# First layer of experts 1 to 6 by fifteen block products for eighteen, with the weight loads of experts 1 to 3 behind the first gathered rows

## The chip, the cores and the metric

The kernel runs on one core of a Trainium2 chip. A core has five engines with an instruction queue each: TensorE (PE, with its weight loads shown apart as PEld), VectorE (DVE), ScalarE (ACT), GpSimd (POOL) and SyncE (SP). Each takes its instructions in order; they wait for each other through semaphores. Matmuls and transposes go to PSUM, eight banks of 128 x 512 floats; everything else on the core lies in SBUF. The metric is the device time of one execution in microseconds (us), as the median of several runs.

## The reference

`x` is 1250 tokens of 768 floats. A graph part (two attention layers over 41,250 edges) and a linear-attention part (`mix`) are added to it; then comes a mixture of eight experts, with the best two of a gate for each token:

```python
x = x + gnn(xn, edges) + mix(xn)          # xn: layer norm of x
t = layernorm(x)
gate = t @ Wg + bg
scores, idx = top_k(gate, 2)
h = gelu(einsum('td,edh->eth', t, W1) + b1)      # W1: 8 x 768 x 384
y = einsum('eth,ehd->etd', h, W2) + b2           # W2: 8 x 384 x 768
comb = sum(one_hot(idx, 8) * scores)
out = x + einsum('te,etd->td', comb, y)
```

All of it is in 32-bit floats. The kernel computes an expert for the tokens that chose it, not for all.

## The kernel before, in words

The parts run one after another: edges and features, six attention heads, keys and values of `mix`, and then a stage over five pairs of token tiles (from about 580 to 865 us) that ends the tokens: queries, output projections, the sum, layer norm and the gate. That stage writes each finished tile twice: to `out`, and, normalised and with its gates, to a buffer in device memory, `xl_d` (L937 and L951). At its end the numbers of the tokens of each expert are known, as columns of `idx` of 128 tokens each (L1049).

The expert stage follows. Each expert gets three columns, 384 tokens, from the code; columns beyond these are handled at the end (`other`). For expert e:

- `gather` (L1060) fetches the rows of three columns from `xl_d` with an indirect DMA on the GpSimd queue each (`xg`, three buffers), turns them with 18 PE transposes into six banks `px`, and copies these to `xsT` on VectorE (L1075). It also copies the gates of the tokens.
- `inner` (L1081) is the first layer: for each of three blocks f of 128 hidden features, six matmuls of 384 columns (weights block stationary, tokens moving) into a bank `ph`, and a gelu with bias on ScalarE to `hT` (L1092). That is 18 matmuls. A 32-bit matmul [...]shows as two records in the profile. Expert 0 is done for its first column alone and then for the other two.
- `give` (L1095), once for each column j, is the second layer: ScalarE multiplies the bias row with the gates (`gb`, two buffers), PE does two halves of three matmuls into two banks `py`, VectorE makes `ys = py * gate + gb` (L1108, two buffers), and an indirect DMA on the GpSimd queue adds the rows to `out` (L1110). Each of these scatter-adds waits for the one before it to land, since they write the same tensor.

In the loop (L1160) the order of the code is: `inner` of e, `gather` of e + 1, three `give` of e, then the loads for later. `spare` holds the second bias rows of two experts; the row of e + 2 is loaded when the last `gb` of e is done (L1175). The weights lie in a ring of four buffers `w` (`expert`, L745, two loads of 1152 KB on the SP queue: first layer L748, second layer L750), shared with the weight matrices of the stage before. Expert 0 takes the first buffer that comes free there; experts 1 to 3 take the others in L1050 and L1051, as the last products of that stage are done with them. The weights of e + 4 are loaded when the second layer of e has been computed (L1177).

PSUM is split into pools: two banks for `px`, two for `ph`, four for `py`.

The order in the queues is not quite that of the code. The framework that builds the program has a scheduler, which moves an instruction ahead of others on its engine where it reckons that the engine would wait otherwise; the matmuls of `py` between the transposes `px` are its work, for instance.

`xnT` (128 x 7500 floats) and `kept` (128 x 7920) hold features and weights of the earlier stages. The expert stage of the kernel before doesn't use them.

Of the kernel before, what the change touches and what calls it, by code (L numbers as in the profile page):

```python
# [27 lines left out]
F32 = mybir.dt.float32  # L28
# [12 lines left out]
KC = D // 128  # L41
# [19 lines left out]
def row_bcast(ap, parts):  # L61

    n = 1
    for s in ap.shape:
        n *= s
    return bass.AP(tensor=ap.tensor, offset=ap.offset, ap=[[0, parts], [1, n]])


@with_exitstack
def gps_block(ctx: ExitStack, tc: tile.TileContext, x, src, dst, norm_g, norm_b, W1, a_src1, a_dst1,  # L70
# [671 lines left out]

    fp = ctx.enter_context(tc.tile_pool(name="fp", bufs=1, side="right"))

    def expert(w1, w2, b2, b):  # L745

        t = wt.tile([128, KC, D], F32, name="w", bufs=4).rearrange("p c f -> p (c f)")
        nc.sync.dma_start(t[:, :KC * FF].rearrange("p (c f) -> p c f", c=KC),  # L748
                          w1.rearrange("(c p) f -> p c f", p=128))
# [18 lines left out]
    with ExitStack() as rs:  # L768
# [290 lines left out]

    def gather(rows, e):  # L1060

        got = []
        for r in rows:
            xg = sp.tile([128, D + NE], F32, name="xg", bufs=3)
            nc.gpsimd.indirect_dma_start(xg, None, xl_d, bass.IndirectOffsetOnAxis(r, 0))
            got.append(xg)
        xT = sp.tile([128, KC, FIX * 128], F32, name="xsT")
        gates = sp.tile([128, FIX], F32, name="gates")
        for j, xg in enumerate(got):
            for a in range(2):  # L1070
                px = x_p.tile([128, 512], F32, name="px")
                for c in range(3):
                    o = (3 * a + c) * 128
                    nc.tensor.transpose(px[:, c * 128:(c + 1) * 128], xg[:, o:o + 128], ident)  # L1074
                nc.vector.tensor_copy(xT[:, 3 * a:3 * a + 3, j * 128:(j + 1) * 128],  # L1075
                                      px[:, :384].rearrange("p (b n) -> p b n", b=3))
            at = slice(D + e, D + e + 1) if isinstance(e, int) else bass.ds(e + D, 1)
            nc.vector.tensor_copy(gates[:, j:j + 1], xg[:, at])
        return xT, gates

    def inner(w, xT, bias, a=0, b=FIX, hT=None):  # L1081

        if hT is None:
            hT = sp.tile([128, FC, FIX * 128], F32, name="hT")
        n = slice(a * 128, b * 128)
        for f in range(FC):
            ph = h_p.tile([128, 512], F32, name="ph")
            for c in range(KC):
                o = c * FF + f * 128
                nc.tensor.matmul(ph[:, n], w[0][:, o:o + 128], xT[:, c, n], start=c == 0,  # L1090
                                 stop=c == KC - 1)
            nc.scalar.activation(hT[:, f, n], ph[:, n], AF.Gelu, bias=bias[:, f])  # L1092
        return hT

    def give(w, hT, j, rows, gates):  # L1095
# [4 lines left out]
        ys = sp.tile([128, D], F32, name="ys")  # L1100
        for k in range(2):
            half = slice(k * 384, (k + 1) * 384)
            py = y_p.tile([128, 512], F32, name="py")
            for f in range(FC):
                o = KC * FF + f * D + k * 384
                nc.tensor.matmul(py[:, :384], hT[:, f, j * 128:(j + 1) * 128], w[:, o:o + 384],  # L1106
# [44 lines left out]
    for vals, add, row in ((place, float(NV), v_row), (which, 0.0, e_row)):  # L1151
        pick = fp.tile([128, NE], F32, name="pick", bufs=2)
        nc.vector.tensor_mul(pick, vals, mine)
        one = fp.tile([128, 1], F32, name="one", bufs=2)
        nc.vector.tensor_reduce(one, pick, AX.X, ALU.add)
        pr = h_p.tile([128, 512], F32, name="ph")
        nc.tensor.transpose(pr[:1, :128], one, ident)
        nc.vector.tensor_scalar(row, pr[:1, :128], add, None, op0=ALU.add)

    for e in range(NE - 1):  # L1160
        xT, gates = ahead
        bias = fb1T[:, :, e:e + 1]
        if e:
            hT = inner(ring[e], xT, bias)
        else:
            hT = inner(ring[e], xT, bias, 0, 1)
            inner(ring[e], xT, bias, 1, FIX, hT)
        ahead = gather(fixed(e + 1), e + 1)
        if e == NE - 2:
            ee, more_rows, more_bias, more_w = first  # L1170
            more_xT, more_gates = gather([more_rows], ee)
        for j, rows in enumerate(fixed(e)):
            give(ring[e], hT, j, rows, gates[:, j:j + 1])
        if e + 2 < NE:
            nc.sync.dma_start(spare[e % 2], row_bcast(fb2[e + 2], 128))  # L1175
        if e + 4 < NE:
# [53 lines left out]
```

## Time and profile before

| | |
|---|---|
| Median of 3 runs | 1097.52 us (1096.05 to 1099.54) |
| The profiled execution's own time | 1097.82 us |
| Its span, first to last instruction | 1096.1 us |
| PE busy, share of the span | 1031.0 us, 94% |
| VectorE busy | 705.8 us, 64% |
| ScalarE busy | 359.9 us, 33% |
| GpSimd busy | 78.8 us, 7% |
| DMA, over the span | 79.51 MB, 73 GB/s |

In the expert stage alone, from 901.00 to 926.50 us (one expert): PE 25.50 us of 25.50, VectorE 6.91, ScalarE 4.55, GpSimd 7.67, DMA 202 GB/s.

Names of tiles in the profile are those of the code, without buffer numbers. `L1090` is line 1090 of the kernel before. A group line has the count, the busy time with the mean of one in ns, and the idle time of the engine just before these instructions with what ended it. `SPq` is the queue of DMA issues of SyncE. The granted clock of PE is given as a share of full speed. The chain of work that ended last is followed backwards from the last instruction, at each step to what released it.

### The profile page before, as it was taken

How to read it: one execution, taken by the hardware profiler on the slowest of the kernel's cores; microseconds unless marked ns; L12 is line 12 of the kernel's file. 1: busy time of each engine (PE TensorE's matmuls, PEld its weight loads, DVE VectorE, ACT ScalarE, POOL GpSimd, SP SyncE). 2: the span in 40 equal slices, each digit the busy share in tenths (PEclk: the TensorE clock that was granted, in tenths of full speed). 3: DMA queues.
4: the chain of work that ended last, by engine and by line, in shares of the span. 5: the costliest groups of instructions: out<-in, count | busy, mean ns of one | idle time of the engine just before them, and what ended most of it. 6: DMA issues, size and time to landing. Idle time of an engine off the chain costs nothing.

```text
span 1096.1 us, 12392 instructions
## 1 busy us (share of the span) xinstructions
PE 1031.0 (94%) x4630; PEld 701.6 (64%) x4630; DVE 705.8 (64%) x1460; ACT 359.9 (33%) x548; POOL 78.8 (7%) x106
## 2 busy tenths in 40 slices
PE   6999999999999999988999999999999499999996
PEld 5876666587878879544555555656665376666674
DVE  7866684697897957769687958686855522222321
ACT  4612226372728373283833121112110111111121
POOL 2000000000000000000001000000000122223321
PEclk9999999999999999999999999999999699999998
DMA  5060000000000002000035002021144847777534
GB/s 161 29 211 19 29 15 1 1 1 1 1 1 1 1 1 87 1 0 1 15 142 153 1 15 71 20 65 43 58 153 132 274 116 221 213 213 203 116 58 59
DMA packets 35412, 79.51 MB, mean 73 GB/s; under 512 B 7078, under 2 KB 15416, under 8 KB 35348
## 3 DMA queue, kind: packets, MB, share of 16 engines
q1 hardware_dynamic: 29588, 58.90, 16.8%
q0 software_dynamic: 5760, 19.78, 8.5%
q8 instruction: 37, 0.61, 0.2%
q14 instruction: 27, 0.22, 0.1%
HBM read 60.33 MB, written 18.34 MB: 72 GB/s over the span
## 4 chain that ended last, share of the span: by engine, by line
PE 73%; DVE 20%; DMA 2%; ACT 1%; issue 1%; POOL 0%; DVEq 0%; POOLq 0%; ACTq 0%
PE s L863 19%; PE mm L648 9%; PE ph L1090 9%; PE py L1106 8%; PE mm L477 8%; DVE scr L569 6%; DVE w L589 5%; DVE w L590 5%; PE ag L602 3%; PE mm L924 2%; PE ag L624 2%; PE ec L398 2%; PE mm L452 2%; PE px L1074 2%; PE rb L558 1%; PE mm L662 1%
## 5 line engine op out<-in xcount | busy, mean ns | idle before, releaser
L602 PE MATMUL ag<-kept,w 125*125 125x198 f32 x800 | 137.5, 333 | 5.1 <-DVE w L590 4.8
L602 PEld LDWEIGHTS ag<-kept,w 125*125 125x125 f32 x800 | 133.5, 188 | 9.0 <-DVE w L590 9.0
L1106 PE MATMUL py<-w,hT 128*128 128x384 f32 x300 | 100.9, 486 | 0.0
L1090 PE MATMUL ph<-xsT,w 128*128 128x384 f32 (+2 forms) x432 | 99.9, 390 | 0.0
L589 DVE TENSOR_TENSOR w<-v,w 125x1250 f32<-125x1250 f32 x60 | 86.3, 1453 | 6.0 <-ACT w L587 5.4
L648 PE MATMUL mm<-Wv_sb,xnT 128*125 128x384 f32 x240 | 85.6, 489 | 4.8 <-DVE kvacc L668 4.8
L1090 PEld LDWEIGHTS ph<-xsT,w 128*128 128x128 f32 x432 | 68.9, 191 | 30.3
L569 DVE CUSTOM_DVE_ANT_0 scr<-ss_row,mask 125x1250 bf16<-125x1250 f32 x60 | 87.2, 1453 | 1.6 <-ACT ss_row L560 1.2
L477 PE MATMUL mm<-Wg,xnT 128*125 128x400 f32 x240 | 87.7, 505 | 0.2 <-ACT xnT L367 0.2
L590 DVE SCALAR_TENSOR_TENSOR w<-w,AT 125x1250 f32<-125x1250 f32 x60 | 86.4, 1454 | 0.4
L588 ACT ACTIVATE v<-dn_row,sl 125x1250 f32<-125x1250 f32 x60 | 79.3, 1333 | 17.4 <-DVE w L589 16.9
L648 PE MATMUL mm<-Wk_sb,xnT 128*125 128x384 f32 x240 | 85.0, 487 | 0.0
L1108 DVE SCALAR_TENSOR_TENSOR ys<-py,gates,gb 128x384 f32<-128x384 f32 x50 | 30.3, 616 | 79.3 <-PE py L1106 54.7
L1106 PEld LDWEIGHTS py<-w,hT 128*128 128x128 f32 x300 | 55.1, 190 | 33.1
L1075 DVE COPY xsT<-px 128x384 f32<-128x384 f32 x50 | 25.8, 552 | 73.3 <-PE px L1074 73.3
L648 PEld LDWEIGHTS mm<-Wv_sb,xnT 128*125 128x125 f32 x240 | 42.5, 187 | 31.4 <-DVE kvacc L668 6.9
L477 PEld LDWEIGHTS mm<-Wg,xnT 128*125 128x125 f32 x240 | 42.5, 188 | 26.5 <-ACT xnT L367 0.9
L1099 ACT ACTIVATE gb<-spare,gates 128x768 f32<-128x768 f32 x24 | 22.4, 935 | 112.4 <-DVE ys L1108 94.8
L587 ACT ACTIVATE w<-up_row,s 125x1250 f32<-125x1250 f32 x40 | 53.2, 1331 | 17.7 <-PE ag L602 17.6
L648 PEld LDWEIGHTS mm<-Wk_sb,xnT 128*125 128x125 f32 x240 | 42.0, 187 | 22.7 <-issue 1.8
L863 PE MATMUL s<-w,xnT 128*125 128x384 f32 x150 | 55.4, 489 | 0.0
L863 PE MATMUL s<-w 128*125 128x384 f32 x150 | 53.9, 491 | 0.0
(328 smaller groups left out, 1515.1 us busy)
## 6 DMA issues: line engine op xcount, KB each, us to landing
w<-in_L_ffn_W_dram SPq DMA_DIRECT2D x18, 1152.0 KB
xt<-in_x_dram SPq DMA_DIRECT2D x20, 336.0 KB
out_dram<-xt SPq DMA_DIRECT2D x10, 336.0 KB
xl_d<-xl SPq DMA_DIRECT2D x10, 336.0 KB
spare<-in_L_ffn_b_dram SPq DMA_DIRECT2D x8, 384.0 KB
W_sb<-in_L_gnn_W_dram SPq DMA_DIRECT2D x1, 2304.0 KB
Wk_sb<-in_L_mix_Wk_dram SPq DMA_DIRECT2D x1, 2304.0 KB
Wv_sb<-in_L_mix_Wv_dram SPq DMA_DIRECT2D x1, 2304.0 KB
```

Source lines behind the costliest of these rows:

```text
L477: nc.tensor.matmul(ps[:PT, :2 * (CG + 2)], xnT[:, c, t * PT:(t + 1) * PT], Wg1[:, c, 2 * k:2 * k + 2].rearrange("p h c -> p (h c)"), start ...
L569: nc.vector.tensor_tensor_reduce(scr, ss_row, mask[:, t], 1.0, 0.0, ALU.mult, ALU.max, top[:, t:t + 1])
L587: nc.scalar.activation(w, up_row, AF.Exp, bias=ss[:, st:st + 1])
L588: nc.scalar.activation(v, dn_row, AF.Exp, bias=sl[:, st:st + 1])
L589: nc.vector.tensor_tensor(w, v, w, op=ALU.max)
L590: nc.vector.scalar_tensor_tensor(w, w, 2.0, AT[:, st, :N], op0=ALU.min, op1=ALU.mult)
L602: nc.tensor.matmul(ag[:, t // 2, o:o + CG], w[:, t * PT:(t + 1) * PT], gw[:, st, hd], start=st == 0 and t % 2 == 0, stop=st == NT - 1, ski ...
L648: nc.tensor.matmul(ps[:PT, :384], xnT[:, c, t * PT:(t + 1) * PT], w[:, c, half], start=c == 0, stop=c == KC - 1)
L863: nc.tensor.matmul(ps, left[:, c], right[:, c], start=start and c == 0, stop=c == n - 1, skip_group_check=True)
L1090: nc.tensor.matmul(ph[:, n], w[0][:, o:o + 128], xT[:, c, n], start=c == 0, stop=c == KC - 1)
L1106: nc.tensor.matmul(py[:, :384], hT[:, f, j * 128:(j + 1) * 128], w[:, o:o + 384], start=f == 0, stop=f == FC - 1)
L1108: nc.vector.scalar_tensor_tensor(ys[:, half], py[:, :384], gates, gb[:, half], op0=ALU.mult, op1=ALU.add)
```

## The change

Split the first layer of an expert into blocks: W1, transposed, is 3 x 2 blocks (three blocks of 128 hidden features, two halves of 384 input features), and the gathered tokens are 2 x 3 (two halves of input features, three columns of 128 tokens). The plain product of these takes 18 products of blocks, each of them three matmuls. The change does it with fifteen: eleven sums and differences of the weight blocks (`WAYS[0]`) and eleven of the token blocks (`WAYS[1]`) are made first, each 128 x 384 floats; each product multiplies one block or sum of weights by one of tokens; and the nine blocks of the result are sums of products (`PRODUCTS`).

- `weight_sums` and `token_sums` make the sums on VectorE. They lie in 33 slots of `xnT` and `kept`: two sets of eleven for weights, one for tokens.
- `inner15` does the products, three matmuls of 128 columns each (L1124 of the kernel after). Five of the fifteen are added onto a bank that already holds another product. A product's first use in a block of `hT` is a copy on ScalarE (`=`, or `=-` with the sign turned), each further one an addition or subtraction on VectorE from the bank. When all is done, three gelus run over `hT` in place. It is called for experts 1 to 6; experts 0 and 7, and the columns at the end, keep `inner`.
- The `xsT` copies of experts 1 to 7 go from VectorE to ScalarE.
- The three PSUM pools of the stage become one, `e_p`, of eight banks in turn.
- The loads of experts 1 to 3 are issued behind the gather of expert 0: VectorE first copies a gathered gate into two elements of the buffer, so that the load of that buffer waits for the copy.

In the code, the sums for the weights of e + 1 stand between the products of e, those of expert 1 between the `give` of expert 0, and the token sums of e + 1 ahead of the `give` of e. In the program as built, the scheduler has moved the weight sums of one expert up: those of experts 1 and 2 both stand in expert 0's part, those of e + 2 between the products of e for e = 1 to 4, and none between those of 5 and 6.

```diff
+WAYS = ((("12", 5, 1, 6), ("13", 3, 1, 4), ("9", 1, -1, "13"), ("14", 3, -1, 1), ("15", 2, -1, "12"),
+         ("7", 1, 1, "15"), ("3", 2, -1, 6), ("8", 4, 1, 5), ("-2", 2, 1, "9"), ("1", 5, -1, 3),
+         ("5", 6, -1, 4)),
+        (("4", 5, -1, 2), ("2", 4, 1, 6), ("9", "2", -1, 3), ("14", 1, -1, "9"), ("7", 1, 1, 2),
+         ("11", 6, -1, 3), ("15", "7", -1, 5), ("3", "15", -1, 4), ("8", 3, -1, 5), ("1", 3, -1, 2),
+         ("5", 6, -1, 5)))
+PRODUCTS = (
+    ("6", None, 1, 1, (1, "="), (2, "=-")),
+    ("10", None, 2, 4, (1, "+"), (3, "=-"), (7, "=")),
+    ("12", None, "12", 5, (8, "="), (9, "=")),
+    ("4", None, 5, "4", (8, "-"), (5, "=-")),
+    ("9", None, "9", "9", (4, "=-"), (3, "-")),
+    ("14", "6", "14", "14", (4, "+")),
+    ("13", None, "13", 3, (3, "+"), (6, "=")),
+    ("7", "12", "7", "7", (2, "+")),
+    ("11", None, 4, "11", (4, "-"), (6, "+"), (9, "+")),
+    ("3", "4", "3", "3", (7, "+")),
+    ("8", None, "8", "8", (5, "-")),
+    ("2", None, "-2", "2", (3, "+")),
+    ("15", None, "15", "15", (2, "-"), (7, "-")),
+    ("1", "13", "1", "1", (5, "+")),
+    ("5", "8", "5", "5", (9, "+")))
...
-    def expert(w1, w2, b2, b):
+    def expert(w1, w2, b2, b, behind=None):
         t = wt.tile([128, KC, D], F32, name="w", bufs=4).rearrange("p c f -> p (c f)")
+        if behind is not None:
+            nc.vector.tensor_copy(t.rearrange("p (a f) -> p a f", a=2)[:1, :, 0],
+                                  behind.to_broadcast([1, 2]))
...
-        for e in range(1, 4):
-            ring.append(expert(fW1[e], fW2[e], fb2[e] if e < 2 else None, spare[e % 2]))
...
-    x_p = ctx.enter_context(tc.tile_pool(name="x_p", bufs=2, space=PSUM))
-    h_p = ctx.enter_context(tc.tile_pool(name="h_p", bufs=2, space=PSUM))
-    y_p = ctx.enter_context(tc.tile_pool(name="y_p", bufs=4, space=PSUM))
+    e_p = ctx.enter_context(tc.tile_pool(name="e_p", bufs=8, space=PSUM))
+    q3 = KC // 2
+    places = [xnT.rearrange("p c n -> p (c n)"), kept]
...
+    def inner15(A, B, bias, between):
+        hT = sp.tile([128, FC, FIX * 128], F32, name="hT")
+        C = [hT[:, i, j * 128:(j + 1) * 128] for i in range(3) for j in range(3)]
+        banks = {}
+        for name, onto, a, b, *uses in PRODUCTS:
+            ps = banks[name] = banks[onto] if onto else bank()
+            for c in range(q3):
+                nc.tensor.matmul(ps[:, :128], A[a][:, c], B[b][:, c], start=c == 0 and not onto,
+                                 stop=c == q3 - 1, skip_group_check=True)
+            for to, how in uses:
+                to = C[to - 1]
+                if how == "=":
+                    nc.scalar.copy(to, ps[:, :128])
...
+            if between:
+                between.pop(0)()
...
+        for f in range(FC):
+            nc.scalar.activation(hT[:, f], hT[:, f], AF.Gelu, bias=bias[:, f])
+        return hT
...
     ahead = gather(fixed(0), 0)
+    for e in range(1, 4):
+        ring.append(expert(fW1[e], fW2[e], fb2[e] if e < 2 else None, spare[e % 2],
+                           ahead[1][:1, e - 1:e]))
...
+        between = []
+        if 0 < e < NE - 2:
+            A, between = weight_sums(ring[e + 1], e + 1)
         if e:
-            hT = inner(ring[e], xT, bias)
+            hT = inner15(now, B, bias, between)
+            now = A
...
-        ahead = gather(fixed(e + 1), e + 1)
+        ahead = gather(fixed(e + 1), e + 1, nc.scalar.copy)
+        todo = []
+        if e < NE - 2:
+            B, todo = token_sums(ahead[0])
+        if e == 0:
+            now, between = weight_sums(ring[1], 1)
+        for make in todo:
+            make()
...
             give(ring[e], hT, j, rows, gates[:, j:j + 1])
+            for make in between[j * 6:(j + 1) * 6]:
+                make()
```

More of the change, by code (lines that the diff above doesn't have):

```diff
@@ L1060, in gather, with bank, sums, make @@
-    def gather(rows, e):
+    e_p = ctx.enter_context(tc.tile_pool(name="e_p", bufs=8, space=PSUM))
+    q3 = KC // 2
+    places = [xnT.rearrange("p c n -> p (c n)"), kept]
+    slot3 = lambda k: places[k % 2][:, k // 2 * q3 * 128:(k // 2 + 1) * q3 * 128].rearrange(
+        "p (c n) -> p c n", c=q3)
+    def bank():
+        return e_p.tile([128, 512], F32, name="ps")
+    def sums(blocks, side, at):
+        got = {k + 1: b for k, b in enumerate(blocks)}
+        todo = []
+        for k, (name, a, sign, b) in enumerate(WAYS[side]):
+            got[name] = slot3(at + k)
+            def make(name=name, a=a, sign=sign, b=b):
+                op = nc.vector.tensor_add if sign > 0 else nc.vector.tensor_sub
+                op(got[name], got[a], got[b])
+            todo.append(make)
+        return got, todo
@@ new lines, in weight_sums, with token_sums @@
+    def weight_sums(w, e):
+        v = w[0][:, :KC * FF].rearrange("p (g c f) -> p g c f", g=2, c=q3)
+        return sums([v[:, g, :, i * 128:(i + 1) * 128] for i in range(3) for g in range(2)], 0,
+                    e % 2 * len(WAYS[0]))
+    def token_sums(xT):
+        return sums([xT[:, g * q3:(g + 1) * q3, j * 128:(j + 1) * 128] for g in range(2)
+                     for j in range(3)], 1, 2 * len(WAYS[0]))
+    def inner15(A, B, bias, between):
[11 more added lines that the diff above has]
+                    nc.scalar.copy(to, ps[:, :128])
+                elif how == "=-":
+                    nc.scalar.mul(to, ps[:, :128], -1.0)
+                elif how == "+":
+                    nc.vector.tensor_add(to, to, ps[:, :128])
+                else:
+                    nc.vector.tensor_sub(to, to, ps[:, :128])
+            if between:
+                between.pop(0)()
+        while between:
+            between.pop(0)()
+        for f in range(FC):
+            nc.scalar.activation(hT[:, f], hT[:, f], AF.Gelu, bias=bias[:, f])
+        return hT
@@ L1062, in gather @@
+    def gather(rows, e, copy=nc.vector.tensor_copy):
         got = []
@@ L1070, in gather @@
             for a in range(2):
-                px = x_p.tile([128, 512], F32, name="px")
+                px = bank()
                 for c in range(3):
@@ L1074, in gather @@
                     nc.tensor.transpose(px[:, c * 128:(c + 1) * 128], xg[:, o:o + 128], ident)
-                nc.vector.tensor_copy(xT[:, 3 * a:3 * a + 3, j * 128:(j + 1) * 128],
-                                      px[:, :384].rearrange("p (b n) -> p b n", b=3))
+                copy(xT[:, 3 * a:3 * a + 3, j * 128:(j + 1) * 128],
+                     px[:, :384].rearrange("p (b n) -> p b n", b=3))
             at = slice(D + e, D + e + 1) if isinstance(e, int) else bass.ds(e + D, 1)
@@ L1086, in inner @@
         for f in range(FC):
-            ph = h_p.tile([128, 512], F32, name="ph")
+            ph = bank()
             for c in range(KC):
@@ L1102, in give @@
             half = slice(k * 384, (k + 1) * 384)
-            py = y_p.tile([128, 512], F32, name="py")
+            py = bank()
             for f in range(FC):
@@ L1155, in gps_block @@
         nc.vector.tensor_reduce(one, pick, AX.X, ALU.add)
-        pr = h_p.tile([128, 512], F32, name="ph")
+        pr = bank()
         nc.tensor.transpose(pr[:1, :128], one, ident)
@@ L1167, in gps_block @@
             inner(ring[e], xT, bias, 1, FIX, hT)
-        ahead = gather(fixed(e + 1), e + 1)
+        ahead = gather(fixed(e + 1), e + 1, nc.scalar.copy)
+        todo = []
+        if e < NE - 2:
[4 more added lines that the diff above has]
+            make()
         if e == NE - 2:
```

## The prediction

> **What bounds the kernel now.** First the chain of work that ended last, in order of time, through the expert stage (start, us, what):
>
> ```profile
> 852.25 5.45 DMA xl_d<-xl
> ...
> 865.48 6.42 DMA xg<-xl_d,idx
> ...
> 926.50 11.61 PE ph L1090 x36
> 938.11 0.66 PE px L1074 x6
> ...
> 941.40 10.32 PE py L1106 x32
> ```
>
> From about 872 us on every piece is PE work: `ph` (first layer), `px` (18 transposes), `py` (second layer). Starts of `ph`, 901.27 and 926.50, give a period of 25.22 us per expert: 11.61 + 2.0 + 11.61. So PE alone is the bound there. Ahead of it two transfers are on the chain.
>
> Next one period of the timeline (start, us, engine and line, then idle time and releaser), for what runs beside PE with little room:
>
> ```profile
> 944.92 1.61 POOL L1110 DMA_INDIRECT out_dram<-ys,idx  x1 [2.14 <-DVE ys L1108]
> 945.69 0.34 SPq L1175 DMA_DIRECT2D spare<-in_L_ffn_b_dram  x1
> ...
> 951.75 0.37 SPq L748 DMA_DIRECT2D w<-in_L_ffn_W_dram  x1
> ...
> 952.21 1.14 DVE L1108 SCALAR_TENSOR_TENSOR ys<-py,gates,gb 128x384 f32<-128x384 f32 x2 [3.70 <-DMA out_dram<-ys,idx]
> ```
>
> `ys` has two buffers, so the third `ys` of an expert waits on VectorE until the first scatter-add has landed, 3.70 us here. Nothing PE needs stands behind it yet. The landing times of the three scatters of this expert (issued 944.92, 952.88, 962.40):
>
> ```profile
> DMA to landing us min/median/max: 7.2/7.2/7.2
> ...
> DMA to landing us min/median/max: 8.8/8.8/8.8
> ...
> DMA to landing us min/median/max: 5.5/5.5/5.5
> ```
>
> The third has no load beside it, the first has the 384 KB `spare` load issued 0.77 us after it, the second a whole pair of weight loads. Last, the groups by form, for prices:
>
> ```profile
> L678 DVE TENSOR_TENSOR kvacc<-kvacc,pair 128x128 f32<-128x128 f32 x6 | 1.6, 287 | 0.0
> ...
> L858 DVE TENSOR_TENSOR zS<-qT,zS 128x375 f32<-128x375 f32 x5 | 2.7, 549 | 0.1
> ```
>
> **Part 1, the products.** Removed per expert: 18 matmuls of 384 columns, 36 records[...], 11.61 us, 0.3225 a record. Added: 15 products of 3 matmuls of 128 columns, 90 records. The 128-column form of L1090 runs at 2.01 / 18 = 0.1117 us a record in expert 0 (chain, 876.54), so 10.05 us. PE per expert falls from 25.22 to 23.66 us; for experts 1 to 6 that is -9.4 us if PE stays the bound.
>
> **Part 2, what feeds them.** VectorE gets 22 sums of 128x384 (row above 0.55; two in a row of the same size take 1.01 on L1018, so 0.50 in a queue, bounds 0.46 and 0.55) and 16 additions of a 128x128 bank into `hT` (no PSUM row of that size; 0.287 is nearest, 0.23 to 0.29 in a queue). It loses six `xsT` copies, which go to ScalarE at 0.48 (L734, same size from PSUM). ScalarE also gets nine 128x128 copies at 0.27 (L726). VectorE comes to 11 + 4.2 + 3.7 (six `ys`) + 0.4 = 19 us of 25: it fits as a total. What decides is the order in its queue. In the built program VectorE has, per expert: additions of the products with 8 weight sums between, 3 weight sums, 11 token sums of the next expert, `ys` of tile 0, 1, 2, three gate copies, additions again. ScalarE has `gb` of the next expert's second tile behind the first two product copies, and that `gb` waits for the third `ys` to free its buffer.
>
> **Part 3, the ring that this closes.** Count from the first `py` matmul of an expert, in its order:
> - the last addition ends about then; gelu of the third row block and five `xsT` copies hold token sums back to +1.7; 11 sums at 0.50, 5.5, and two `ys` halves at 0.6 (L1108): first scatter at +8.4 (today 944.92 against 941.24, +3.7);
> - it lands. The `spare` load still follows it by 0.8. The weight load, freed when `py` ends at +11.65, now comes 3.25 us after it instead of 6.8, so 7.2 is a lower value for a landing with `spare`, 8.8 the one under weights, 5.5 the one beside nothing. I take 8.0 between the first two; 5.5 to 8.8 for the range;
> - third `ys`, two halves: 1.25;
> - ScalarE: `gb` 0.935, then four 128x128 copies out of banks at 0.27: 2.05. PE has meanwhile done seven products and stands: the eighth ("7") goes onto the bank of "12", which these copies read;
> - eight products left, 48 records: 5.36; 18 transposes: 2.0; latencies 0.1. Next `py`.
>
> Sum 8.4 + 8.0 + 1.25 + 2.05 + 5.36 + 2.0 + 0.1 = 27.2, against 25.22: +2.0 per expert; the saving of part 1 is inside a wait. Five such periods (`py` of expert 1 to that of 6): +10.0. With landings of 5.5 or 8.8 they give -2.5 or +14; the queue price of a sum (0.46 or 0.55) moves them by 2 to 3 more. The experts without weight sums between the products (5, 6) gain nothing by it: there PE's eight products fill the time.
>
> **Part 4, the loads that wait.** Six loads (7.1 MB) leave 840 to 866 and are issued behind the first gathered rows, on SP, with nothing of the mix stage queued behind them any more. Then the next to last `xl_d` write lands sooner and `xl` (L358) loses its 0.9 us wait; the last write, issued at 859.48 and so landing at about 865.4 today, is no longer what releases the gather, but `idx` on VectorE (863.47, so 862.6). Gather issued 2.6 us earlier, and landing in 3.7 (the least landing of a gather in this stage) to 6.42; I take 3.9: another 2.5. First rows 5.1 us earlier, at 866.8.
>
> **Part 5, expert 0.** Ahead of the first-layer weights of expert 2 in the queues, they included, stand three halves of 1.18 MB, a bias row of 0.39 and gathers of about 2.0, 5.9 MB; issued at 867.2, flowing 1.7 later (840.33 to 842 in the windows) at the 0.4 MB a us that 844 to 846 moved, they are there at about 883.7. In the built program VectorE does the weight sums of experts 1 and 2 (waiting for these) ahead of the token sums and of `ys`: 883.7 + 5.5 + 5.5 + 1.2 and 0.2 to the issue: first scatter at 896.1, landing 8.8 under the loads, then 1.25 + 2.05 + 5.36 + 2.0: `py` of expert 1 at 915.6, ending 11.6 later at 927.2. It ends at 926.5 today: +0.7, and the 5.1 us are spent. If the weights come in time for VectorE the sum is -4, if gathers and loads slow each other +5.
>
> **Hidden.** Three 1x2 copies that hold the loads cost 0.15 each on VectorE (L1078), in the wait for gathers. One pool of eight banks for three pools: six `py` and six `px` stay in it, the stall that it brings is in part 3. Copies of `xsT` on ScalarE lie under PE's transposes and first `py`; they are late only for the token sums (counted). Tail behind expert 6: 0.
>
> **A rule weighed.** The windows (PE busy, ..., clock, DMA share, GB/s), where PE had thin work and then none:
>
> ```profile
> 857.00:858.00 1.00, 0.20 (x1) 0.10 (x1) 0.10 (x2) 0.00 (x0) 0.00 (x0) 1.00 0.91 347
> 858.00:859.00 1.00, 0.00 (x0) 0.00 (x0) 0.97 (x4) 0.00 (x0) 0.00 (x0) 0.50 1.05 393
> ```
>
> Within 1 us of its last matmul (857.2) PE is at half clock, and it stays there until 3 to 4 us after 871.95. The Trainium skill (TensorE: Matmul & The Clock Gate, "What's actually happening") says that it takes a whole idle window of about 3.4 us, free-running, and as long a busy one to come back. My stall is +16.3 to +19.7, 3.4 us. By the row, where thin work had come before, every stall could halve the clock: 5.36 us of products last 1.7 longer, five times: +8.5. By the rule, after full work, a window hardly fits: 0. PE is full until the stall, so I take 0 and keep +8.5 for the range.
>
> **Sum.** The profiled execution took 1097.82 (span 1096.1 and 1.7 around it): 1097.8 + 0.7 + 10.0 = 1108.5. The median of the runs is 1097.52, 0.3 lower: 1108.
>
> **Rivals.**
> - *PE stays the bound* (the change does what it says): VectorE and the scatter keep up, 23.66 a period, and the early rows count: 1097.8 - 9.4 - 5.1 = 1083. Against it: the 3.70 us wait with the additions now queued behind it. Chance 0.05.
> - *Faster by the scatter alone*: the ring stands, but the first scatter lands beside next to nothing. Each us of landing is a us of each period, which equals 25.22 at 6.0. At 5.5 the sum is 1097.8 + 0.7 - 2.5 = 1096; below 5.2 it is faster by over 0.3%, or below 6.1 where expert 0 has its weights in time (-4): 1094 to 1090, say 1092. For it: 5.5 is measured. Against: `spare` is still issued right behind it. Chance 0.11.
> - *Even*: landings of 5.7 to 6.6, or 7.2 with expert 0 in time: 1095 to 1101. Chance 0.11.
> - *The clock falls in the stalls*, or the landing is 8.8 and expert 0 late: 1116 to 1122. Chance 0.15.
> - My ring: 0.58, 1101 to 1116.
>
> **Numbers.** 1108. About 0.3%, 3.3 us, is what a measurement of this kernel tells from no change. Faster 0.16, same 0.11, slower 0.73. Range: 1092 (scatter quick, weights in time) to 1119 (8.8, half of the clock cost).
>
> **What would show it.** Period of `py` starts about 27 for experts 1 to 6; the third `ys` waiting on the scatter with additions behind; PE idle 2 to 4 us in the middle of each fifteen products, released by ScalarE; first scatter some 8 us behind the first `py`; gather issued near 862.8. Wrong if PE is gapless over an expert, if the first scatter lands in under 6 us, or if VectorE's sums in a queue take under 0.4.

## The result and the profile after

The kernel after takes 1105.80 us (median of 8 runs, 1103.52 to 1112.23) against 1098.95 us before (8 runs beside it, 1096.05 to 1104.62). The ratio is 1.0067, with a 95% interval of 1.0045 to 1.0089: slower by 0.67%. The profiled execution took 1105.47 us, its span is 1103.7 us (before 1097.82 and 1096.1).

First the chain of work that ended last, of the kernel after, in order of time (start, us, what):

```profile
864.13 4.44 DMA xg<-xl_d,idx
...
869.41 14.36 DMA w<-in_L_ffn_W_dram
883.80 0.56 DVE xnT L1102
...
895.54 8.05 DMA out_dram<-ys,idx
904.24 0.62 DVE ys L1192
904.95 0.94 ACT gb L1183
...
906.59 8.17 PE ps L1124 x48
...
1041.08 4.58 DMA xg<-xl_d,rows
...
1047.32 13.94 PE ps L1190 x36
```

Before, the chain was PE from expert to expert. Now it runs over a load of weights, the sums on VectorE, a scatter, the third `ys`, `gb`, and only then eight products on PE, and so on for each expert. At the end stands something that the prediction doesn't have: a gather of the extra column (`xg<-xl_d,rows`) and a slow second layer behind it.

One period, of expert 3, in the timeline of the kernel after (start, us, engine and line, then idle time and releaser):

```profile
966.48 11.78 PE L1190 MATMUL ps<-w,hT 128*128 128x384 f32 x36
972.75 2.29 DVE L1192 SCALAR_TENSOR_TENSOR ys<-ps,gates,gb 128x384 f32<-128x384 f32 x4
974.16 1.61 POOL L1194 DMA_INDIRECT out_dram<-ys,idx  x1 [1.45 <-DVE ys L1192]
974.94 0.34 SPq L1276 DMA_DIRECT2D spare<-in_L_ffn_b_dram  x1
978.29 0.37 SPq L778 DMA_DIRECT2D w<-in_L_ffn_W_dram  x1
981.89 1.14 DVE L1192 SCALAR_TENSOR_TENSOR ys<-ps,gates,gb 128x384 f32<-128x384 f32 x2 [6.85 <-DMA out_dram<-ys,idx]
983.13 0.94 ACT L1183 ACTIVATE gb<-spare,gates 128x768 f32<-128x768 f32 x1 [3.72 <-DVE ys L1192]
984.77 0.94 PE L1124 MATMUL ps<-xnT,kept 128*128 128x128 f32 x6 [1.82 <-ACT hT L1129]
990.23 2.13 PE L1158 MATMUL ps<-ident,xg 128*128 128x128 f32 x18
```

The third `ys` waits 6.85 us for the first scatter (3.70 in the period shown of before), `gb` waits for it, and PE stands 1.82 us at the eighth product until ScalarE has emptied the bank. The ring of part 3 is there, link by link. But the period from `py` to `py` is 25.72 us here and 24.66, 25.27 and 25.24 for the others, not 27.2.

PE at expert 6, in the timeline of the kernel after:

```profile
1039.99 2.13 PE L1158 MATMUL ps<-ident,xg 128*128 128x128 f32 x18
1045.80 1.51 PE L1158 MATMUL ps<-ident,xg 128*128 128x128 f32 x6 [3.69 <-DMA xg<-xl_d,rows]
1047.11 14.15 PE L1190 MATMUL ps<-w,hT 128*128 128x384 f32 x36
```

and windows of the same stretch (PE busy, ..., granted clock, DMA share, GB/s):

```profile
1044.00:1045.00 1.00, 0.00 (x0) 0.00 (x0) 0.00 (x0) 0.00 (x0) 0.00 (x0) 1.00 0.54 224
...
1046.00:1048.00 2.00, 2.00 (x8) 1.69 (x8) 1.11 (x2) 0.00 (x0) 0.00 (x0) 0.50 0.03 8
...
1052.00:1053.00 1.00, 1.00 (x4) 0.57 (x3) 0.00 (x0) 0.00 (x0) 0.00 (x0) 1.00 0.00 0
```

PE stands 3.69 us before the six transposes of the extra column, and from about 1045.1 to 1051.9 (windows of half a us) it has half its clock: 36 records of `py` take 14.15 us where the same 36 take 11.78 in every other expert.

The time between the same places of the two traces, in us, from starts in PE's timeline. A: from the first product of the token stage (576.88 before, 576.67 after) to the first transpose of expert 0. B: to the first layer of expert 1. C: to that of expert 2. D: to that of expert 6, a fourth of it. E: to the transposes behind it. F: to the first layer of expert 7. G: to the last group of `py`.

| | A | B | C | D (4 of these) | E | F | G |
|---|---|---|---|---|---|---|---|
| before | 295.07 | 29.16 | 25.23 | 25.22 | 11.61 | 15.30 | 27.69 |
| after | 290.28 | 29.75 | 31.47 | 25.22 | 10.94 | 21.11 | 27.68 |
| difference | -4.79 | +0.59 | +6.24 | 4 x 0.00 | -0.67 | +5.81 | -0.01 |

The differences make +7.2; what lies ahead (-0.2) and behind (+0.6) makes the +7.6 of the span. So the loss isn't in the periods of experts 2 to 6: they are even. It is in expert 1 (C) and behind expert 6 (F), and the early rows (A) pay for most of C.

### The profile page after: what moved, and what is told of

Read it like the earlier page. It is cut to its first block, busy times and chain, and to the rows that moved or that the text cites. A ratio compares the mean times of both kernels' runs of the same rounds, so it can differ in the third digit from the quotient of the medians.

```text
span 1103.7 us, 13353 instructions
## 1 busy us (share of the span) xinstructions
PE 1028.1 (93%) x4954; PEld 727.2 (66%) x4954; DVE 767.0 (69%) x1649; ACT 386.5 (35%) x644; POOL 83.3 (8%) x106
## 4 chain that ended last, share of the span: by engine, by line
PE 60%; DVE 25%; DMA 7%; ACT 3%; issue 2%; POOL 0%; DVEq 0%; POOLq 0%; ACTq 0%
PE s L893 19%; PE mm L674 9%; PE mm L503 7%; DVE scr L595 6%; DVE w L615 5%; DVE w L616 5%; DMA out_dram<-ys,idx 5%; PE ag L628 3%; PE mm L954 2%; PE ag L650 2%; DVE xnT L1102 2%; PE ps L1190 2%; PE ec L424 2%; PE ps L1124 2%; DVE kept L1102 2%; PE mm L478 2%
## 5 line engine op out<-in xcount | busy, mean ns | idle before, releaser
L1190 PE MATMUL ps<-w,hT 128*128 128x384 f32 x300 | 100.8, 495 | 0.0
L1190 PEld LDWEIGHTS ps<-w,hT 128*128 128x128 f32 x300 | 57.5, 194 | 38.3 <-issue 2.2
L1192 DVE SCALAR_TENSOR_TENSOR ys<-ps,gates,gb 128x384 f32<-128x384 f32 x50 | 29.1, 611 | 76.8 <-DMA out_dram<-ys,idx 40.7
L431 DVE TENSOR_TENSOR AT<-AT,ec 125x120 f32 x162 | 44.6, 275 | 10.6 <-PE ec L424 7.7
L650 PE MATMUL ag<-w,h 125*97 125x417 f32 (+1 forms) x120 | 46.7, 532 | 4.8 <-DVE w L616 4.8
L1194 POOL DMA_INDIRECT out_dram<-ys,idx x24 | 40.2, 1675 | 136.3 <-DVE ys L1192 79.2
```

What stands on the lines that cost most here:

```text
L431: nc.vector.tensor_add(here, here, ec[:, g])
L650: nc.tensor.matmul(ag[:, i, :b - a], h2[:, st, hd * (C2 + 1):(hd + 1) * (C2 + 1)], w[:, a:b], start=st == 0, stop=st == NT - 1)
```

## The experiments

Two theories of the result stand against each other at first. *Ring*: the third `ys` behind the first scatter holds each expert, as predicted; without it PE would run at 23.7 a period, and the loss is the whole saving. *Tail*: the wait for the extra column's rows and the half clock behind it, which the prediction put at 0. Beside them: what the waiting loads bring. The stages of all profiled executions, in the columns from above:

| | A | B | C | D | E | F | A to G |
|---|---|---|---|---|---|---|---|
| before | 295.07 | 29.16 | 25.23 | 25.22 | 11.61 | 15.30 | 504.9 |
| after | 290.28 | 29.75 | 31.47 | 25.22 | 10.94 | 21.11 | 512.1 |
| e1 extra column later | 290.70 | 31.79 | 26.56 | 25.35 | 11.15 | 14.52 | 503.8 |
| e2 three `ys` | 290.72 | 31.25 | 23.63 | 23.65 | 10.04 | 23.80 | 501.7 |
| e3 before + loads | 289.95 | 35.12 | 25.23 | 25.22 | 11.61 | 15.33 | 505.8 |
| e4 before + one pool | 294.07 | 30.06 | 25.19 | 25.19 | 11.61 | 20.33 | 509.7 |
| e5 `ys` sooner | 291.05 | 31.82 | 25.57 | 24.43 | 11.04 | 21.05 | 505.9 |
| e6 products alone | 297.90 | 29.52 | 24.43 | 25.81 | 10.95 | 19.81 | 513.5 |
| e7 e2 + extra column later | 290.19 | 29.84 | 23.63 | 24.11 | 10.05 | 14.23 | 492.1 |
| e8 e7, loads as before | 298.86 | 30.52 | 23.63 | 23.63 | 10.04 | 14.24 | 499.5 |
| e9 `spare` later | 290.87 | 29.90 | 25.88 | 24.38 | 10.80 | 20.59 | 503.2 |
| e10 plain products, loads, extra column later | 290.85 | 31.27 | 25.19 | 25.19 | 11.61 | 14.24 | 501.6 |
| e11 first layers first | 297.90 | 31.81 | 25.91 | 25.62 | 11.59 | 19.75 | 517.2 |
| e12 e11 + extra column later | 290.71 | 29.76 | 31.32 | 25.41 | 11.98 | 14.51 | 507.6 |

Gains of one version over another are differences of medians below; the ratios to the kernel before, measured beside each version, give the same within 0.9 us. Single executions of one code differ by about 2 us in B, where PE comes out of its half clock sooner or later (first layer of expert 0, 72 records: 11.96 us in the kernel after, 13.08 in e1).

### The tail: e1 and e4

e1, the kernel after with the extra column's gather and transposes behind the first second-layer tile of expert 6 (as built, only the place of these six transposes on PE and of their two copies on VectorE changes):

```diff
-        if e == NE - 2:
-            ee, more_rows, more_bias, more_w = first
-            more_xT, more_gates = gather([more_rows], ee)
         for j, rows in enumerate(fixed(e)):
             give(ring[e], hT, j, rows, gates[:, j:j + 1])
+            if e == NE - 2 and j == 0:
+                ee, more_rows, more_bias, more_w = first
+                more_xT, more_gates = gather([more_rows], ee)
```

> The kernel after, with the gather of the extra column (and its six transposes) placed behind the first second-layer tile of expert 6 instead of ahead of all three. Theory 'tail': in the kernel after, the six late transposes stand ahead of all 36 py records on PE, PE stands 3.69 us for their rows, and half clock follows for some 6 us; expert 6 takes 21.1 us from its transposes to the first layer of expert 7 where the kernel before takes 15.3. With py work in front of them the rows land in time: the stall and the half clock go, -5.8 us, so about 1100 us, and the last scatter 5.8 earlier. Rival 'ring': the loss lies in the five periods before, and the last gather or the scatters then wait elsewhere: no change, 1105 to 1106. My prediction had 0 for this part.

Measured: 1099.42 us (12 runs), against before 1.0009 (0.9992 to 1.0027); 6.4 us under the kernel after. PE's timeline of e1 at the place:

```profile
1040.47 4.04 PE L1190 MATMUL ps<-w,hT 128*128 128x384 f32 x12
1044.60 0.85 PE L1158 MATMUL ps<-ident,xg 128*128 128x128 f32 x6
1045.29 7.91 PE L1190 MATMUL ps<-w,hT 128*128 128x384 f32 x24
```

Twelve records of `py` cover the gather; no wait, no half clock (12 and 24 records last 4.04 and 7.91), and F is 14.52 for 21.11. In this execution the tail is worth 6.6 us, and it goes by order alone. (B and C together are 58.4 here and 61.2 in the kernel after with the same order there: PE came to the stall of expert 1 later, stood 2.66 us for 5.03, and kept its clock.)

e4, the kernel before with its three PSUM pools made one:

```diff
-    x_p = ctx.enter_context(tc.tile_pool(name="x_p", bufs=2, space=PSUM))
-    h_p = ctx.enter_context(tc.tile_pool(name="h_p", bufs=2, space=PSUM))
-    y_p = ctx.enter_context(tc.tile_pool(name="y_p", bufs=4, space=PSUM))
+    e_p = ctx.enter_context(tc.tile_pool(name="e_p", bufs=8, space=PSUM))
...
-                px = x_p.tile([128, 512], F32, name="px")
+                px = e_p.tile([128, 512], F32, name="ps")
```

> The kernel before, with only its three PSUM pools made one of eight banks. In the program as built the 18 transposes of an expert, and the 24 of expert 6, then stand in one row ahead of py. Theory 'tail': this alone brings the stall at expert 6 and the half clock behind it: +5.8, about 1105 us, all of it at the end, with periods of 25.2 before it. Rival: the stall comes from the products (late transposes or a late gather there), and the one pool costs nothing: 1099.

Measured: 1099.96 us (20 runs), 1.0021 (1.0008 to 1.0033). PE's timeline of e4, and a window of it:

```profile
1038.61 2.13 PE L1072 MATMUL ps<-ident,xg 128*128 128x128 f32 x18
1043.74 1.51 PE L1072 MATMUL ps<-ident,xg 128*128 128x128 f32 x6 [3.01 <-DMA xg<-xl_d,rows]
1045.05 14.05 PE L1104 MATMUL ps<-w,hT 128*128 128x384 f32 x36
```

```profile
1042.00:1043.00 1.00, 0.00 (x0) 0.00 (x0) 0.01 (x1) 0.00 (x0) 0.00 (x0) 0.91 0.71 292
```

With two `px` banks the transposes had to wait for copies, and the scheduler filled that with `py`; with eight banks all 24 stand in a row ahead of `py`, and those of the last column meet a gather that has just been issued. The profiled execution has the whole loss in F (+5.0), but the median rises by only 1.9. The mean granted clock of each execution tells two kinds apart: sixteen of the twenty have 0.984 to 0.986 (51 of 55 executions of the kernel before have 0.984 to 0.987) and take 1098.27 to 1101.09 us, the other four, the profiled one among them, have 0.979 to 0.983 and take 1103.21 to 1108.18. So most executions of e4 seem to keep their clock behind the wait; that the four lost it at this place is shown for the profiled one alone.

### The ring: e2, e5, e9

e2, the kernel after with a third `ys` buffer; the order in the queues stays the same:

```diff
-        ys = sp.tile([128, D], F32, name="ys")
+        ys = sp.tile([128, D], F32, name="ys", bufs=3)
```

> The kernel after, with three buffers for ys instead of two, so that the third ys of an expert doesn't wait for the first scatter to land. Theory 'ring': the wait for the scatter is what holds PE in the middle of the fifteen products; without it the six stalls (11.0 us in sum, 5.03 of them in expert 1, which also brings 2.6 us of half clock) go, periods of expert 2 to 6 fall from 25.2 to PE's own 23.7, in sum -13.6, about 1092 us. Rival 'VectorE or the chain of scatters takes over': the sums on VectorE, or three scatters one after the other at 8.1 us each, leave the period at 25 or more; then only expert 1 gains, -3 at most, 1103 or above.

Measured: 1096.05 us (20 runs), 0.9974 (0.9962 to 0.9986). PE's timeline of e2 over one period, and at expert 6:

```profile
960.08 11.78 PE L1190 MATMUL ps<-w,hT 128*128 128x384 f32 x36
971.70 1.50 PE L1124 MATMUL ps<-xsT,w 128*128 128x128 f32 x12
...
981.74 2.13 PE L1158 MATMUL ps<-ident,xg 128*128 128x128 f32 x18
983.71 11.78 PE L1190 MATMUL ps<-w,hT 128*128 128x384 f32 x36
```

```profile
1037.60 1.51 PE L1158 MATMUL ps<-ident,xg 128*128 128x128 f32 x6 [6.48 <-DMA xg<-xl_d,rows]
```

PE has no gap in any product, and the period is 23.63: the price of part 1 (25.22 - 11.61 + 10.05 = 23.66) was right. From the first transpose of expert 0 to those of expert 6 it takes 159.5 us against 173.0, the 13.6 expected within 0.1. The third `ys` behind the first scatter is the cause of the stalls in C and D. The time doesn't fall by as much (9.8), since the tail grows: F is 23.80. The gather of the extra column now stands on the GpSimd queue behind the third scatter of expert 5, so PE waits 6.48 us for its rows instead of 3.69.

e5, the kernel after with the first `ys` ahead of the token sums in the code:

```diff
-        for make in todo:
-            make()
...
             give(ring[e], hT, j, rows, gates[:, j:j + 1])
+            if j == 0:
+                for make in todo:
+                    make()
```

> The kernel after, with the first ys of an expert in the code ahead of the token sums; as built, its second half stands ahead of the last four of the eleven token sums on VectorE, so the first scatter is issued 4 x 0.47 = 1.9 us earlier and nothing else changes. Theory 'ring': each us by which the first scatter is earlier takes a us from the stall of PE, until PE is the bound at 23.7: 1.5 a period from 25.2, and in expert 1 the stall of 5.03 shrinks to about 3.1, which may also spare its 2.6 us of half clock: -7.5 to -10, 1096 to 1098 us. Rival: something else in the queues (the order of additions and copies behind) sets 25.2: no change, 1105 to 1106.

Measured: 1100.96 us (7 runs), 1.0031 (1.0009 to 1.0053); 4.8 under the kernel after, where 7.5 to 10 were expected. D falls by 0.8, not 1.5. The GpSimd queue in the timeline of e5:

```profile
938.01 1.95 POOL L1194 DMA_INDIRECT out_dram<-ys,idx  x1 [8.25 <-DMA out_dram<-ys,idx]
944.56 2.11 POOL L1194 DMA_INDIRECT out_dram<-ys,idx  x1 [0.49 <-issue]
```

`ys` was ready sooner, but the first scatter of an expert stands behind the third of the one before and three gathers, 6.55 us in all, and is issued with no wait but the queue's own. In the kernel after this queue had 1.45 us and more to spare ahead of the first scatters of experts 1 to 4. It is the next bound, close behind. More of the gain of this execution is in B and C together (57.4 for 61.2): the stall of expert 1 is 1.68 us for 5.03, and PE keeps its clock there.

e9, the kernel after with the `spare` load held behind the third `ys`:

```diff
+            nc.vector.tensor_copy(spare[e % 2][:1, :1], ys[:1, :1])
             nc.sync.dma_start(spare[e % 2], row_bcast(fb2[e + 2], 128))
```

> The kernel after, with the load of the next second bias row (spare, 384 KB) held behind the first half of the third ys of the expert by a 1x1 copy on VectorE: it is then issued after the first scatter has landed instead of 0.8 us behind its issue. Tests the landing term of the ring. Theory: the first scatter then lands in about 5.5 us (the value of a scatter beside nothing) instead of 7.2 to 7.6, the third ys comes 1.7 earlier, and the stalls of PE (0.63 to 1.82 in experts 2 to 6, 5.03 in expert 1) shrink by as much: periods fall to 23.7 to 24, -1.2 a period and -1.7 to -4.3 in expert 1, in sum some -6 to -8: about 1099. Rival: the weights' loads, issued 4 us behind the first scatter, hold its landing at 7 and over, or the GpSimd queue (third scatter, three gathers, first scatter) takes over: less than -2, 1104 to 1106.

Measured: 1099.77 us (20 runs), 1.0004 (0.9990 to 1.0019); 6.0 under the kernel after, as expected. The timeline of e9:

```profile
943.95 1.61 POOL L1194 DMA_INDIRECT out_dram<-ys,idx  x1 [1.45 <-DVE ys L1192]
949.73 0.62 DVE L1192 SCALAR_TENSOR_TENSOR ys<-ps,gates,gb 128x384 f32<-128x384 f32 x1 [4.88 <-DMA out_dram<-ys,idx]
950.60 0.34 SPq L1278 DMA_DIRECT2D spare<-in_L_ffn_b_dram  x1
```

From the issue of the first scatter to the third `ys` it is 5.78 us (7.31 for the same expert in the kernel after), close to the 5.5 that the third scatter of before took beside no load. The second scatter pays, with a landing of 10.5 beside `spare` and the weights. D falls by 0.84 a period, and B and C together fall by 5.4 (55.8 for 61.2), with a stall of 1.99 us in expert 1 and the clock kept.

### The loads and expert 0: e3, e6, e10, e11, e12

e3, the kernel before with the waiting loads alone (the diff is that of `expert` and its calls in the change):

> The kernel before, with only the second part of the change: the loads of experts 1 to 3 are issued behind the first gathered rows. Theory (part 4 of the prediction): the first rows are there 5.1 us earlier (gather issued at 862.8, landing about 3.9), PE is the bound from there on and nothing needs these weights early, so the whole 5.1 come through: about 1094 us against 1099. Rival: the loads now go beside the gathers of expert 1 and the first scatters, and something waits for them (the first layer of expert 1 near 896, or rows of expert 1): 1098 to 1100, no change.

Measured: 1098.51 us (12 runs), 1.0005 (0.9985 to 1.0024): nothing. A falls by 5.1, as part 4 said, and B rises by 6.0. The timeline of e3:

```profile
870.69 0.94 POOL L1066 DMA_INDIRECT xg<-xl_d,idx  x1 [2.25 <-PE px L1075]
...
879.60 1.08 PE L1075 MATMUL px<-ident,xg 128*128 128x128 f32 x5 [3.67 <-DMA xg<-xl_d,idx]
```

In its queue PE has transposes of expert 1 ahead of most of expert 0's first layer. Their gather, now beside the weight loads, lands in 8.2 us (3.7 before), and PE waits 3.67 for it and comes back at half clock (0.50 from 880 to 882).

e6, the kernel after with the loads in their old place:

```diff
+        for e in range(1, 4):
+            ring.append(expert(fW1[e], fW2[e], fb2[e] if e < 2 else None, spare[e % 2]))
...
-    for e in range(1, 4):
-        ring.append(expert(fW1[e], fW2[e], fb2[e] if e < 2 else None, spare[e % 2],
-                           ahead[1][:1, e - 1:e]))
```

> The kernel after, with the loads of experts 1 to 3 in their old place (no wait for the gathered rows): the products alone. By the traces so far the first rows then come about 4 us later against the work before them (gather 1.7 later, landing 2.4 longer), and the weight sums of experts 1 and 2 no longer wait for weights. Theory (part 5 of the prediction): the token sums of expert 1 then follow the xsT copies directly; first scatter at some 898.5 instead of 895.5, so +3, about 1109 us. Rival: the early rows are spent whole on the wait for the weights of expert 2: within 1 us of the kernel after, 1105 to 1107. A second rival: the weight sums, now on VectorE in the stage before, hold that stage up: 1112 and more.

Measured: 1107.74 us (4 runs), 1.0087 (1.0069 to 1.0105); 1.9 over the kernel after. The sums on VectorE (line L1104 there) in the token stage, one group of six:

```profile
L1104 DVE TENSOR_TENSOR kept<-w x7: 540/555/560, 847.5 to 868.6; 128x384 f32<-128x384 f32 x7
```

Since their weights are there early, the scheduler puts the 22 sums of experts 1 and 2 into the end of the token stage, from 847.5 on, among the work that `idx` needs. A becomes 297.90, 2.8 over the kernel before and 7.6 over the kernel after. Without the wait for weights C is 24.43 for 31.47. The second rival had the mechanism and the first came nearest to the sum: the two nearly cancel.

D of this execution (25.81) has a loss of the clock in it. The eighth product of expert 3, and the one behind it:

```profile
989.33 1.10 PE L1126 MATMUL ps<-xnT,kept 128*128 128x128 f32 x6 [2.13 <-ACT hT L1131]
990.22 1.49 PE L1126 MATMUL ps<-kept,w 128*128 128x128 f32 x6
```

PE was busy up to 987.19 and stood 2.13 us. The granted clock is 1.00 in the wait, 0.98 from 989 to 990 and 0.50 from 990 to 993, and the eight products take 7.09 us for 5.46.

e10, the kernel after with the 18 plain products, two `ys` buffers and copies of `xsT` on VectorE; the one pool and the waiting loads stay, and the extra column comes behind two tiles.

```diff
-        if e:
-            hT = inner15(now, B, bias, between)
-            now = A
+        if e:
+            hT = inner(ring[e], xT, bias)
```

> The kernel after with the plain first layer (18 products, no sums, copies of xsT on VectorE, two ys buffers), the one pool of eight banks, the waiting loads, and the extra column's transposes behind two second-layer tiles of expert 6. In the kernel before with the waiting loads alone, PE took back the gain by 3.67 us of waiting for rows of expert 1 ahead of the first layer of expert 0; with the one pool those transposes stand behind it. Theory: the early rows then come through, 4 to 5 us: 1094 us; and the fifteen products are worth the rest, about 9, to the 1085 of e7. Rival: the loads beside the gathers and the first scatters cost it elsewhere: 1098 to 1099.

Measured: 1093.68 us (12 runs), 0.9963 (0.9938 to 0.9989). The early rows come through where nothing of expert 1 stands ahead of expert 0: A falls by 4.2 and B rises by only 2.1 (6.0 in e3). Another 1.1 is in F and comes from the place of the extra column, not from the loads; no run has this order with the loads in their old place, so how the gain divides between the two is read from the stages of one execution.

e11, the kernel after with the three first-layer loads ahead of the three second-layer ones, and e12, the same with e1's order:

```diff
+        nc.sync.dma_start(t[:, :KC * FF].rearrange("p (c f) -> p c f", c=KC),
+                          fW1[e].rearrange("(c p) f -> p c f", p=128))
...
+    for e in range(1, 4):
+        nc.sync.dma_start(ring[e][0][:, KC * FF:].rearrange("p (c d) -> p c d", c=FC),
+                          fW2[e].rearrange("(c p) d -> p c d", p=128))
```

> The kernel after, with the first-layer weights of experts 1, 2 and 3 issued ahead of the second-layer weights of all three (the waits for the gathered rows as they are). Tests part 5 of the prediction: the weights of expert 2, landed at 883.8, hold VectorE and so the first scatter and expert 1. Theory: they land some 4 us earlier, VectorE does the 22 weight sums without the 1.5 us wait in between, the first scatter comes 1.7 earlier, and the stall of 5.03 in expert 1 shrinks to about 3.3: -1.7, or up to -4.3 if PE then keeps its clock: 1101.5 to 1104. Rival: the sums or the copies themselves are the limit there: 1105 to 1106, no change.

> The kernel of e1 (extra column's transposes behind one tile) with the first-layer weights of experts 1 to 3 first, as in e11. In the profiled execution of e11 the stage behind expert 0's first rows was 2.6 us shorter than in the kernel after and the stall in expert 1 was 2.02 for 5.03, but the execution lost some 7 us at half clock near 596 us, far ahead of the change, and its times (1106.9) don't show the gain. Theory: the weights of expert 2 do hold expert 1 and that clock loss is chance: against e1's 1099.4, -2.6 to -3.5, so 1096 to 1097, and a stall near 2 in expert 1 with full clock behind it. Rival: the order of the loads costs elsewhere what it gains in expert 1 (gathers beside the loads, rows of expert 0): 1099 to 1100.

Measured: e11 1106.88 us (6 runs), 1.0063 (1.0037 to 1.0090); e12 1101.79 us (22 runs), 1.0031 (1.0020 to 1.0043), 2.4 over e1. My theory falls. VectorE no longer waits for weights there, but the GpSimd queue of e12 shows a new wait:

```profile
884.77 4.28 POOL L1149 DMA_INDIRECT xg<-xl_d,idx  x1 [11.40 <-PE ps L1158]
889.36 4.91 POOL L1149 DMA_INDIRECT xg<-xl_d,idx  x1 [0.30 <-DVE xnT L1102]
894.57 0.95 POOL L1149 DMA_INDIRECT xg<-xl_d,idx  x1 [0.30 <-issue]
895.83 1.63 POOL L1194 DMA_INDIRECT out_dram<-ys,idx  x1 [0.31 <-DVE ys L1192]
```

Two gathers of expert 2 take 4.28 and 4.91 us to issue (0.96 to 1.11 in the kernel after). The first scatter's `ys` is done at 894.5, 1.3 us sooner against the first rows than in the kernel after, but the scatter comes out of this queue only at 895.83, 28.3 us behind the first rows, where it comes at 28.6 in the kernel after. B and C together are 61.1 in e12 and 61.2 in the kernel after, 57.7 in e11 and 58.4 in e1: what tells these apart is not the order of the loads but, for the most part, whether PE lost its clock in expert 1 (stalls of 4.95 and 5.03, against 2.02 and 2.66).

### Both faults mended: e7 and e8

e7 is e2 with the extra column behind two tiles (`j == 1` in the diff of e1); e8 is e7 with the loads of e6.

> The kernel after with three ys buffers and the extra column's transposes behind two tiles of the second layer of expert 6. With three buffers alone PE ran gapless in periods of 23.63 but stood 6.48 us for the extra column's rows at expert 6 and ran at half clock behind. Theory: both faults are separate and their costs add: 9.3 us off the run with three buffers (51.5 to 42.2 from the transposes of expert 6 to the last py records), about 1087 us, 1% under the kernel before. Rival: with the earlier PE the last gathers and scatters are late instead, so that at most half of it comes: 1091 to 1093.

> The kernel of e7 (three ys buffers, extra column later), with the loads of experts 1 to 3 in their old place. What the waiting loads are worth once nothing but PE is the bound. Theory: the rows of expert 0 come about 4 us later and PE is gapless behind them, so +4 against e7: about 1091. Rival (as the loads alone did on the kernel before): what is gained ahead is lost again in expert 0 beside the loads: equal to e7 within 1 us.

Measured: e7 1085.07 us (4 runs, 1083.89 to 1085.68), 0.9885 (0.9867 to 0.9902); e8 1091.29 us (15 runs), 0.9934 (0.9917 to 0.9950). PE's timeline of e7 at expert 6:

```profile
1028.02 7.91 PE L1190 MATMUL ps<-w,hT 128*128 128x384 f32 x24
1035.77 0.82 PE L1158 MATMUL ps<-ident,xg 128*128 128x128 f32 x6
1036.42 4.04 PE L1190 MATMUL ps<-w,hT 128*128 128x384 f32 x12
```

The costs add: F is 14.23, and over the five experts of C and D PE stands once, 1.38 us. This version beats both kernels, the one before by 1.15%. The waiting loads are worth 6.2 us in it, more than the 4 expected, because without them the sums again hold up the token stage (A 298.86, in an execution 3.5 us above the median of e8). Against e10 the products, with their third `ys`, are worth 8.6, where part 1 had 9.4 for PE alone.

## Why the prediction was right, and where it was wrong

The sign was right, and 1108 against 1105.8 looks close. The parts were not: two large errors, the ring 10.7 too dear and the tail 5.8 too cheap, went against each other, so that the sum came close is luck.

- **Part 1, products.** Right: 10.05 us for 90 records, and 23.63 a period in e2 for 23.66.
- **Part 2, order on VectorE.** Right in what stands behind what. The sums' queue price was 0.47 (0.50 taken, 0.46 to 0.55 given).
- **Part 3, ring.** Right in mechanism and in each link; e2 and e9 show it. Wrong in size: +10.0 was predicted for five periods, and they came out at 25.22 on average, even with before (with E, -0.7). In the period shown: first scatter at +7.68 (8.4), landing to the third `ys` 7.73 (8.0), `ys` 1.24 (1.25), `gb` and copies 1.64 (2.05), products 5.46 (5.36), transposes 1.97 (2.1): 25.72 for 27.2. The terms that failed are the first scatter (`xsT` copies held the sums to +1.07, not +1.7, and eleven sums took 5.20 for 5.5) and the four bank copies, which follow one another at 0.16 to 0.19 where I took their 0.27 of busy time each. The landing, for which I gave 5.5 to 8.8, was 7.2 to 7.6, near the lower value that I had named for one with `spare` and not taken. Three terms, each erring by 0.3 to 0.7 to the slow side, made 1.5 in this period; the three other periods given above were another 0.4 to 1.1 shorter. That the ring comes out at just the old period is chance: its links have nothing to do with the price of the 18 plain products.
- **The stall** was to be 3.4 us in each expert. It was 0.63 to 1.82 in experts 2 to 6, at the eighth product, released by ScalarE, as said.
- **Part 4, early rows.** Gather at 862.77 (862.8 predicted), rows at 866.78 (866.8); A 4.8 shorter for 5.1. Over the kernels with waiting loads and without the half clock of e11, A is 290.0 to 291.1; in the two that have the old loads and no sums in that stage (before, e4) it is 295.07 and 294.07. So 4 is nearer the truth than 5.
- **Part 5, expert 0.** Weights at 883.77 (883.7), first scatter 895.54 (896.1). `py` of expert 1 ended at 928.17 (927.2). The step that failed is the eight products behind the stall: 8.00 us, not 5.36, since the stall was 5.03 us here and PE came back at half clock. The other terms were 0.4 to 0.6 too long and hid part of it. That VectorE's wait for the weights of expert 2 sets the first scatter is only half the matter: e11 and e12 took that wait away, and the gathers' issue took its place.
- **Hidden: "One pool of eight banks for three pools", and "Tail behind expert 6: 0".** Wrong, and the larger half of the loss: +5.8 in F. I had looked at what the pool does inside the ring and not at the wait of 0.83 us for the same rows in the trace of before, which said that this gather was just covered by `py` in between:

```profile
1043.78 0.85 PE L1074 MATMUL px<-ident,xg 128*128 128x128 f32 x6 [0.83 <-DMA xg<-xl_d,rows]
```

e4 shows that the pool alone brings the longer wait (3.01), e1 that order alone removes it. By the medians e4 loses 1.9 and the kernel after 6.4 (against e1); the wait of the kernel after is 0.7 longer (3.69), and why it costs so much more there is open.
- **The rule weighed.** The Trainium skill (TensorE: Matmul & The Clock Gate, "What's actually happening") asks for a whole idle window of about 3.4 us, and so I took 0. The trace of e6 doesn't agree: 2.13 us of waiting between busy stretches cost the clock there, so a whole idle window of 3.4 isn't needed; the measurement decides. Nor does the length of the wait decide alone: inside the expert stage waits of 2.22 (e12), 2.37 (e11) and 2.66 us (e1) cost no clock, while those of 3.01 to 6.48 all did. The half clock was worth 2.5 in expert 1 (8.00 for 5.46) and 2.4 at expert 6 (14.15 for 11.78): 4.9 of the 7.2 lost, in two places, neither of which is where I had weighed it (five stalls of 3.4).

The rival nearest to what happened is the one that I had called *even*, for the size of the ring (not for its reason: no landing was under 7.2), with the clock rival's cost at two places.

## What to carry to other kernels

When work is put behind a wait in an engine's queue, write the ring out link by link, and take for each link the spacing of such instructions in a queue, not their busy time; then try the cheapest cut, here one more buffer. When pools are merged, look for every place where the small pool had made the scheduler mix two kinds of work, above all where a wait of under 1 us shows that a transfer is only just covered. A gain ahead of a busy stage was kept here only where nothing that the next stage waits for came to stand behind the moved transfers (e10 against e3).

## What was not expected of the hardware

The granted clock does not follow the length of a wait alone. Beside the 2.13 us of e6 and the 2.66 of e1 there is a shorter wait still. In e11 PE stood 1.48 us near 593, far ahead of the change, was busy again from 593.92, and lost half its clock at about 595.7; in e8 the same place had a wait of 1.52 us and kept it. The timeline and windows of e11:

```profile
593.92 3.72 PE L831 MATMUL mm<-Wu_sb,col 96*125 96x384 f32 x8 [1.48 <-ACT w L760]
```

```profile
594.00:595.00 1.00, 1.00 (x4) 0.60 (x5) 1.00 (x2) 0.00 (x0) 0.00 (x0) 1.00 0.33 132
595.00:596.00 1.00, 1.00 (x4) 0.58 (x3) 1.00 (x2) 0.00 (x0) 0.00 (x0) 0.84 0.33 132
596.00:597.00 1.00, 1.00 (x3) 0.34 (x1) 0.88 (x1) 0.00 (x0) 0.00 (x0) 0.50 0.32 129
```

It lasted to about 609, although PE was busy all the time from 593.92 on, and A is 7 us longer in this execution than in others of nearly the same order; so a single profile can carry such a loss by chance. And in e11 and e12 an indirect gather took up to 4.91 us of GpSimd's queue to issue, five times its usual 0.95, so that a scatter can be held in this queue and not only by the landing of the one before it. Why is open: from 884 to 892 the DMA engines are as full in the kernel after (share 1.04 to 1.06, in e12 0.97 to 1.03) and VectorE's sums as dense, and its gathers took 0.96 to 1.11 us there.
